# Moving the token shift of a windowed attention from TensorE to SP's transfers, with the mixture's fronts and the order of the stream set anew

## The chip, the cores and the metric

The kernel runs on one core of a Trainium2 chip. The core has five engines that run at the same time, each through its own instructions in a fixed order: PE (TensorE, matrix products and transposes), DVE (VectorE), ACT (ScalarE), POOL (GpSimd), and SP (SyncE), which here does nothing but issue transfers. An engine waits on semaphores where it needs what another produces. Transfers are carried out by 16 DMA engines beside them. The metric is the device time of one execution in microseconds (us).

## The reference, cut to what matters

The input `x` has 2 batch entries of 1024 tokens with 128 channels, float32. Six blocks follow each other, each added to `x`:

```python
x = x + 0.5 * L0_ffn(layernorm(x))    # mixture of 16 experts, two per token
x = x + L0_attn(layernorm(x))         # full attention, 16 heads of 64
x = x + 0.5 * L0_ffn(layernorm(x))    # the mixture again
x = x + 0.5 * L1_ffn(layernorm(x))    # two layers with windowed attention, below
x = x + L1_attn(layernorm(x))         # linear attention
x = x + 0.5 * L1_ffn(layernorm(x))    # the two layers again
```

The windowed block is what the change touches most. One of its layers reads

```python
def shift_token(t):
    t1, t2 = jnp.split(t, 2, axis=-1)
    t2 = jnp.pad(t2, ((0, 0), (1, 0), (0, 0)))[:, :-1]
    return jnp.concatenate([t1, t2], axis=-1)
...
h = shift_token(x)                    # q, k, v from h; rotary; windows of 64 tokens
x = x + local_attention(q, k, v) @ wo
h = shift_token(x)
h = (h - mean) / sqrt(var + 1e-5) * lg + lb
a, g = split(h @ w1 + b1)
x = x + (a * gelu(g)) @ w2 + b2
```

A token's shifted row has its own channels 0 to 63 and the channels 64 to 127 of the token before it (zeros for the first token of a batch entry). The shift of the second half of the layer is the one at issue.

## The kernel before, in words

**Layout.** `x` and `y` (the stream inside the windowed blocks) stay in SBUF as [128 tokens, 16 tiles, 128 channels], 8 tiles for each batch entry. A group is G = 4 tiles, so a batch entry has two groups (c = 0, 1). The windowed block runs twice, as `local("f0")` and `local("f1")`, with 2 layers x 4 groups each: 16 groups in all, so 16 shifts of the second kind.

**Stages.** First mixture and first attention take some 1000 us in an order that the change leaves alone. Beside the attention's steps POOL builds constants, one every few steps. Then comes the second mixture in 4 chunks of 512 tokens. A chunk has a front (`front_parts`: five pieces of the normalisation, `front_turned` L194, `front_kept` L199, `front_logits` L205, four pieces of `front_gates` from L210 on, `front_weights` L257 to L260) and nine pairs of experts (`entered` L284, `fetched` L292, `gated` L300, `multiplied` L304, `weighted` L308, `left` L268). The fronts of chunks 0 and 1 are done beside the end of the attention; those of chunks 2 and 3 lie in the stream described next.

**The stream.** From the second mixture on the order of all instructions comes from a list: `at(key, fn, ...)` (L950) enters a step with a number, the list is sorted by that number (L1619), and the steps are emitted in that order. Every engine takes its instructions in the order of emission; there is no scheduler behind it. So a table of numbers such as `per_group` is the order of each engine, and a step that is late holds back all that stands behind it on the same engine.

**A group in the windowed attention**, tile by tile: q and k are projected (`project`, L989), squared (L1002, ACT), multiplied by the rotary tables (`cosines` L1010 and `sines` L1021, DVE), summed and scaled (L1035, L1040, POOL), transposed (L1056), kept (L1062). `values` (L1067) and `valued` give v; `valued` stores the windows with two transfers on SP's queue (L1084, L1087: tile `vb` from `vo`). Scores (`attend`, L1100), mask, maximum, exponential, sums and weights (L1112 to L1139) follow, then the upright transposes (`upright`, L1147), the product with v (`weigh`, L1161), the projection (L1177) and the sum into `y` (`added`, L1183, DVE).

Four tiles done, the second half of the layer follows for the group. `lower_half` (L1191) copies channels 0 to 63 of `y` into a new tile `h` on POOL, and for c = 0 saves the last tile's upper channels as `late` for the next group. `shifted` (L1202 to L1205) does the shift on PE, by two or three products with matrices of ones and zeros, into a PSUM bank:

```python
nc.tensor.matmul(sp[:, 0:G, :], lhsT=down_one, rhs=ys[:, :, 64:C], ...)
if c > 0:
    nc.tensor.matmul(sp[:, 0, :], lhsT=last_first, rhs=late[l, b], ...)
nc.tensor.matmul(sp[:, 1:G, :], lhsT=last_first, rhs=ys[:, 0 : G - 1, 64:C], ...)
```

`upper_half` (L1209) copies the bank into `h` on ACT. Then h is normalised in five pieces (`norm_h`): moments on DVE (`bn_stats` L153, `bn_aggr` L155), the negative on POOL, the root on ACT, the offset on POOL, the application on ACT (L141). `inner_turned` (L1224) and what follows is the gated feed-forward, in whose end `outer_added` (L1288, DVE) adds its product `po` to `y`. Groups overlap: while group g is in its second half, the tiles of group g+1 are in their first.

Of the kernel before, what the change touches and what calls it, by code (L numbers as in the profile page):

```python
# [8 lines left out]
F32 = mybir.dt.float32  # L9
# [5 lines left out]
P = 128  # L15
B, S, C = 2, 1024, 128
# [4 lines left out]
NP = E // 2  # L21
# [10 lines left out]
def macaron_kernel(ctx: ExitStack, tc: tile.TileContext, a: dict, out: bass.AP):  # L32
# [835 lines left out]
    def first_weights():  # L868
# [6 lines left out]
        mask, mask0, causal, down_one, last_first = (  # L875
            w1a.tile([P, P], F32, name=nm) for nm in ("mask", "mask0", "causal", "down_one", "last_first")
# [20 lines left out]
                lambda: zero(down_one, 0.0),  # L897
                lambda: select(down_one, [[-1, P]], 1, 1, ne, 1.0),
                lambda: zero(last_first, 0.0),
                lambda: select(last_first[:, 0:1], [[0, 1]], -(P - 1), 1, ne, 1.0),  # L900

# [15 lines left out]
        shapes.extend([mask, mask0, causal, down_one, last_first, hblk, hgrp, hcol])  # L917

    attention0()
    mask, mask0, causal, down_one, last_first, hblk, hgrp, hcol = shapes  # L920
# [36 lines left out]
    def tiles_of(b, c):  # L957
        return b * TB + G * c
# [7 lines left out]
    def local(name, steps, normed, store):  # L966
# [221 lines left out]
        def lower_half(l, b, c):  # L1188
            ys = y[:, tiles_of(b, c) : tiles_of(b, c) + G, :]
            h = work.tile([P, G, C], F32, tag="h", name=f"h_{name}{l}{b}{c}")  # L1190
            nc.gpsimd.tensor_copy(h[:, :, 0:64], ys[:, :, 0:64])  # L1191
            if c == 0:
                late[l, b] = small.tile([P, 64], F32, tag=f"late{b}", name=f"late_{name}{l}{b}", bufs=1)
                nc.gpsimd.tensor_copy(late[l, b], ys[:, G - 1, 64:C])
            mids[l, b, c] = h

        def shifted(l, b, c):


            ys = y[:, tiles_of(b, c) : tiles_of(b, c) + G, :]  # L1200
            sp = ps_["h", l, b, c] = bankT(f"sh_{name}{l}{b}{c}").rearrange("p (k d) -> p k d", d=64)
            nc.tensor.matmul(sp[:, 0:G, :], lhsT=down_one, rhs=ys[:, :, 64:C], start=True, stop=False)  # L1202
            if c > 0:
                nc.tensor.matmul(sp[:, 0, :], lhsT=last_first, rhs=late[l, b], start=False, stop=False)
            nc.tensor.matmul(sp[:, 1:G, :], lhsT=last_first, rhs=ys[:, 0 : G - 1, 64:C], start=False, stop=True)  # L1205

        def upper_half(l, b, c):
            h = mids[l, b, c]
            nc.scalar.copy(h[:, :, 64:C], ps_.pop(("h", l, b, c))[:, 0:G, :])  # L1209
            mids[l, b, c] = h, norm_pieces(h, G, f"f{name}{l}{b}{c}", h)  # L1210
# [74 lines left out]
        def outer_added(l, b, c):  # L1285
# [5 lines left out]
            (-0.473, project), (-0.424, squares), (-0.249, cosines), (-0.183, sines), (0.096, least_norm),  # L1291
            (0.281, summed), (0.449, roots), (0.625, scaled), (0.834, turned), (0.880, kept),
            (1.214, attend), (1.218, masked), (1.742, lowered), (1.772, values), (1.865, valued),
            (2.038, raised), (2.216, totals), (2.464, weights), (2.737, upright), (2.777, stood),
            (3.084, weigh), (3.277, out_kept), (3.646, out_projected), (3.730, added),
        ]
        per_group = [
            (-0.203, lower_half), (0.205, shifted), (0.287, upper_half), (0.402, norm_h, 0),
            (0.701, norm_h, 2), (0.892, norm_h, 1), (1.199, norm_h, 3), (1.332, norm_h, 4),
            (1.625, inner_turned), (1.670, inner_kept), (2.276, second_bias), (2.397, gates),  # L1300
            (2.411, gelus), (2.511, third), (3.716, others), (3.934, first_two), (4.423, outer),
            (4.497, outer_added),
        ]
        for (l, b, c), n0 in steps.items():
            if l == 0:
                for part, d in enumerate(normed[b, c]):
                    at(d, norm, b, c, part)
            at(n0 - (0.786 if l == 0 else 2.722), channels, l, b, c)
            at(n0 + 0.749, keys_of_group, l, b, c)
            for k in range(G):  # L1310
                for d, fn in per_tile:
                    at(n0 + k + d, fn, l, b, G * c + k)
            for d, fn, *more in per_group:
                at(n0 + 7 + d, fn, l, b, c, *more)
            if l == 1:
                at(n0 + 11.568, onto_x, b, c, store)
# [16 lines left out]
    def linear_attention(starts):  # L1333
# [215 lines left out]
        def result(b, n):  # L1549
# [7 lines left out]
            (-0.327, norm, 0), (-0.133, norm, 1), (-0.117, norm, 2), (-0.075, norm, 3), (0.127, norm, 4),  # L1557
            (0.336, turned), (0.403, out_bias), (0.422, project, 2), (0.464, biased, 2),
            (0.504, project, 0), (0.568, biased, 0), (0.632, moments), (0.755, deviations),
            (0.874, inverted), (0.975, offsets),  # L1560
        ]
        per_tile = [
            (0.087, standard), (0.151, padded), (0.253, upright), (0.318, features), (0.374, spread),
            (0.592, keys_back), (0.620, scores, 1), (0.688, second_half), (0.890, cut), (1.118, scores, 0),
            (1.144, sums), (1.296, first_half), (1.303, summed), (1.407, numerators), (1.449, divided),
            (1.687, result), (2.068, moved),
# [13 lines left out]
    def mixture_at(chunks, fronts):  # L1580

        front_table = (
            -17.085, -13.072, -16.449, -1.888, 9.442, 10.794, 14.341, 21.404, 22.809, 28.561, 34.790,
            46.770, 47.680,
        )
        pair_table = [(1.440, fetched), (1.551, entered), (1.573, gated), (1.724, multiplied), (2.045, weighted), (2.197, left)]
        for c, m in chunks.items():
# [4 lines left out]
            at(m + 0.25 * NP + 2.388, finish, c)  # L1592
        for c, m in fronts.items():
            for d, (fn, *more) in zip(front_table, front_parts):
                at(m + d, fn, c, *more)
        return max(e[0] for e in plan)

    chunks = {0: -53.408, 1: -45.379, 2: 19.763, 3: 28.642}
    mixture_end = mixture_at(chunks, {2: -60.469, 3: -24.112})
    at(mixture_end + 0.001, moe_pool.close)  # L1600
    second = []
    at(-52.208, lambda: second.extend(later_weights()))
    at(-44.179, linear_weights)
    for k in range(4):
        at(20.581 + 0.3 * k, lambda k=k: table_scaled(*second, k))
    mixed = {g: [chunks[2 * g[0] + g[1]] + d for d in (4.394, 5.991, 11.199, 12.627, 13.589)] for g in groups}
    steps = {
        (0, 0, 0): 31.511, (0, 0, 1): 35.51, (0, 1, 0): 39.502, (0, 1, 1): 43.494,
        (1, 0, 0): 47.544, (1, 0, 1): 51.537, (1, 1, 0): 55.603, (1, 1, 1): 59.643,
    }  # L1610
    local("f0", steps, mixed, False)
    linear_attention({(0, 0): 59.504, (0, 1): 63.574, (1, 0): 67.587, (1, 1): 71.626})
    steps = {
        (0, 0, 0): 66.682, (0, 0, 1): 70.734, (0, 1, 0): 74.785, (0, 1, 1): 78.807,
        (1, 0, 0): 82.829, (1, 0, 1): 86.879, (1, 1, 0): 90.871, (1, 1, 1): 94.947,
    }
    mixed = {g: [steps[0, *g] + d for d in (-1.347, -1.236, -1.27, -1.04, -0.937)] for g in groups}
# [75 lines left out]
```

## Time and profile before

| what | value |
|---|---|
| median of 3 runs | 1915.93 us (1915.51 to 1917.19) |
| the profiled execution's own time | 1915.74 us |
| its span | 1913.7 us |
| PE, DVE, ACT, POOL busy | 96%, 73%, 59%, 59% of the span |
| mean granted clock of TensorE | 0.987 |

The span runs from the first to the last instruction of the profiled execution[...]. Times in a row of the profile are microseconds from the span's start unless marked ns. A row of the chain of waits has its start, how long it stood, the engine, the tile and the line of the source. A row of a timeline has start, duration, engine and line, and at its end in brackets how long the engine had idled and which instruction released it. A row of a table of stretches has the stretch, its length, the busy time of PE, weight loads, DVE, ACT and POOL (with the number of instructions), TensorE's granted clock as a share of full speed, the mean busy share of the 16 DMA engines (a sum over queues, so it can pass 1), and GB/s. A row of the transfers has the tiles, the queue, how often, the size of each and the median time from issue to landing; the rows for `vb` say 128.0 KB and about 2.2 us.

### The profile page before, as it was taken

The numbers are of one execution on the slowest core, as the hardware profiler recorded it, in microseconds if no ns is written. First come the engines' busy times: TensorE is split into PE (matmuls) and PEld (weight loads), VectorE is DVE, ScalarE is ACT, GpSimd is POOL, SyncE is SP. The second block draws the span as 40 slices with busy tenths as digits, with TensorE's granted clock in tenths as the row PEclk, the third lists the DMA queues.
The fourth block names the chain that finished last, engine by engine and source line by source line (L and its number), as shares of the span: only waits on it lengthen the run. The fifth ranks groups of instructions, "written<-read, shape, count | busy, mean of one in ns | idle before, by whom it ended". The sixth has DMA issues, their size and how long they took to land.

```text
span 1913.7 us, 37577 instructions
## 1 busy us (share of the span) xinstructions
PE 1837.6 (96%) x14482; PEld 1190.3 (62%) x14482; DVE 1401.8 (73%) x2450; ACT 1130.2 (59%) x2083; POOL 1135.1 (59%) x1036
## 2 busy tenths in 40 slices
PE   8999999999999999999999889999999899999997
PEld 5555666566665666656666556666756566666765
DVE  5748677776768677776763568888887788888884
ACT  4325555655566555655653356776767467677765
POOL 4544444343435444353344379888887689788883
PEclk8998999999999999999999899999999999999999
DMA  5330101010101001011023211111100000011110
GB/s 133 107 88 23 23 16 31 12 31 4 34 12 25 21 22 24 12 34 60 2 69 91 68 34 29 26 25 24 27 18 15 7 18 20 19 26 24 26 34 26
DMA packets 52413, 64.13 MB, mean 34 GB/s; under 512 B 17890, under 2 KB 26892, under 8 KB 51980
## 3 DMA queue, kind: packets, MB, share of 16 engines
q1 hardware_dynamic: 52236, 61.74, 12.6%
q8 instruction: 115, 1.88, 0.4%
q14 instruction: 62, 0.51, 0.1%
HBM read 27.89 MB, written 1.31 MB: 15 GB/s over the span
## 4 chain that ended last, share of the span: by engine, by line
PE 67%; DVE 12%; ACT 11%; POOL 4%; issue 4%; DMA 0%; SPq 0%; DVEq 0%; POOLq 0%; ACTq 0%
PE s L650 11%; PE tp L700 10%; PE av L717 9%; ACT p L679 3%; PE qk_f L989 3%; PE gu_m L284 2%; PE pq L598 2%; PE av_f L1161 2%; PE gu_m L285 2%; PE s_f L1100 2%; PE tp_f L1147 2%; PE tq_f L1056 2%; PE acc_m L268 2%; PE v_f L1067 2%; PE po_f L1277 2%
## 5 line engine op out<-in xcount | busy, mean ns | idle before, releaser
L686 POOL TENSOR_SCALAR p<-p,den 128x1024 f32<-128x1024 f32 x256 | 292.3, 1154 | 398.1 <-DVE den L684 316.5
L679 ACT ACTIVATE p<-p,nm 128x1024 f32<-128x1024 f32 x256 | 294.7, 1151 | 357.1 <-DVE nm L666 335.5
L666 DVE CUSTOM_DVE_ANT_0 p<-s,bias 128x1024 f32<-128x1024 f32 x256 | 302.8, 1220 | 103.7 <-PE s L650 102.3
L700 PEld LDWEIGHTS tp<-ident,p 128*128 128x128 f32 x2048 | 226.7, 141 | 99.3 <-issue 38.0
L700 PE MATMUL tp<-ident,p 128*128 128x128 f32 x2048 | 276.9, 278 | 11.7 <-ACT pt L704 10.3
L650 PE MATMUL s<-qk,qk 64*128 64x512 f32 x1024 | 258.3, 618 | 3.8 <-DVE nm L666 3.7
L717 PE MATMUL av<-pt,v 128*64 128x256 f32 x2048 | 249.0, 385 | 0.0
L706 DVE COPY pt<-tp 128x512 f32<-128x512 f32 x256 | 176.3, 689 | 92.6 <-PE tp L700 92.2
L717 PEld LDWEIGHTS av<-pt,v 128*64 128x64 f32 x2048 | 135.8, 136 | 150.1 <-issue 83.7
L1035 POOL TENSOR_TENSOR t_f<-t_f,t_f 128x1024 f32<-128x1024 f32 x64 | 151.0, 2360 | 15.3 <-DVE t_f L1021 12.5
L308 POOL TENSOR_TENSOR h_m<-h_m,cb_m 128x512 f32<-128x512 f32 x64 | 88.1, 1378 | 116.9 <-DVE h_m L304 88.1
L704 ACT COPY pt<-tp 128x512 f32<-128x512 f32 x256 | 147.4, 576 | 4.2 <-PE tp L700 3.9
L650 PEld LDWEIGHTS s<-qk,qk 64*128 64x128 f32 x1024 | 89.2, 186 | 88.3 <-issue 84.8
L1040 POOL TENSOR_TENSOR t_f<-t_f,rn_f 128x1024 f32<-128x1024 f32 x64 | 122.2, 1909 | 23.1 <-ACT rn_f L1031 19.6
L1139 POOL TENSOR_TENSOR s_f<-s_f,sm_f 128x1024 f32<-128x1024 f32 x64 | 121.4, 1898 | 15.9 <-DVE sm_f L1135 12.3
L989 PE MATMUL qk_f<-wqkv,hT 128*128 128x512 f32 x256 | 124.7, 610 | 2.5 <-DVE hh_f L1253 1.2
L1002 ACT ACTIVATE t_f<-qk_f 128x1024 f32<-128x1024 f32 x64 | 65.3, 1021 | 97.8 <-PE qk_f L989 90.4
L1125 POOL TENSOR_TENSOR s_f<-s_f,mx_f 128x1024 f32<-128x1024 f32 x64 | 121.9, 1905 | 0.4 <-DVE mx_f L1120 0.4
L300 ACT ACTIVATE h_m<-gu_m 128x512 f32<-128x512 f32 x72 | 43.0, 597 | 133.2 <-PE gu_m L285 126.5
L304 DVE TENSOR_TENSOR h_m<-h_m,gu_m 128x512 f32<-128x512 f32 x72 | 49.3, 685 | 83.9 <-ACT h_m L300 82.5
L1134 DVE TENSOR_REDUCE sm_f<-s_f 128x8 f32<-128x1024 f32 x64 | 77.9, 1217 | 26.7 <-ACT s_f L1130 26.6
L614 POOL TENSOR_TENSOR rot<-rot,rot 128x512 f32<-128x512 f32 x32 | 40.7, 1272 | 88.0 <-DVE rot L609 88.0
(376 smaller groups left out, 3762.6 us busy)
## 6 DMA issues: line engine op xcount, KB each, us to landing
cb_m<-cwd_m SPq DMA_DIRECT2D x128, 128.0 KB, 3.1
qk<-rot SPq DMA_DIRECT2D x256, 64.0 KB, 2.0
tab<-in_xpos_dram SPq DMA_DIRECT2D x2, 1024.0 KB, 6.7
wqkv<-in_L_ffn_wqkv_dram SPq DMA_DIRECT2D x2, 768.0 KB, 8.2
x<-in_L_attn_x_dram SPq DMA_DIRECT2D x4, 256.0 KB, 3.8
wraw<-in_qkv_wT_dram SPq DMA_DIRECT2D x2, 512.0 KB, 4.3
vb_f<-vo_f SPq DMA_DIRECT2D x8, 128.0 KB, 2.2
out_dram<-x SPq DMA_DIRECT2D x4, 256.0 KB, 2.3
```

Source lines behind the costliest of these rows:

```text
L650: nc.tensor.matmul(pss[r][:, c, :], lhsT=qT[rows[r], t * P : (t + 1) * P], rhs=kT[rows[r], c * 512 : (c + 1) * 512], start=True, stop=True,)
L666: nc.vector.tensor_tensor_reduce(out=s, in0=pss[r].rearrange("p a n -> p (a n)"), in1=bias[r][:, o : o + S], scale=-1.0, scalar=3.0e38, op ...
L679: nc.scalar.activation(s, s, AF.Exp, bias=nm[:, r : r + 1], scale=-1.0, accum_out=den[:, r : r + 1])
L686: nc.gpsimd.tensor_scalar(probs[i, r], probs[i, r], den[:, r : r + 1], 1.0, ALU.mult, ALU.mult)
L700: nc.tensor.transpose(tp[:, k * P : (k + 1) * P], s[:, kb * P : (kb + 1) * P], ident)
L704: nc.scalar.copy(dst, src)
L706: nc.vector.tensor_copy(dst, src)
L717: nc.tensor.matmul(po[r * 64 : r * 64 + 64, 0 : 2 * P], lhsT=v[:, kb, r * 64 : r * 64 + 64], rhs=pts[i // 2, r, g][:, kb - 4 * g, :], star ...
L989: nc.tensor.matmul(ps[:, s, :], lhsT=hTs[b][:, n * P : (n + 1) * P], rhs=lw[l][0][:, s * INNER : (s + 1) * INNER], start=True, stop=True,)
L1035: nc.gpsimd.tensor_tensor(t1, t1, t2, ALU.add)
L1040: nc.gpsimd.tensor_tensor(t3, t3, rn.unsqueeze(2).to_broadcast([P, 2 * HL, 64]), ALU.mult)
L1125: nc.gpsimd.tensor_tensor(s3, s3, mx.unsqueeze(2).to_broadcast([P, HL, P]), ALU.subtract)
```

## The change: what it does, and the diff

1. **The shift by transfers.** `shifted` has no matmuls any more. It issues transfers on SP's queue from `y` straight into `h`: one for rows 0 to 126 of all four tiles to rows 1 to 127 (127 rows, each 4 pieces of 64 floats), and three of a single row, each from the last row of a tile to the first row of the next. For c = 0 a fourth one-row transfer saves the last row of the group as `late`, now one row in place of 128. `lower_half` writes the first row's upper half on POOL: zeros for c = 0, a copy of `late` for c = 1. `upper_half` (the ACT copy) and the constants `down_one` and `last_first` are gone. The moments of h on DVE now read what the transfers write.

2. **The fronts of chunks 2 and 3** get a table of numbers each (`front_tables`) in place of one for both, and other starts. In the new order the transposes and logits of chunk 2 lie inside chunk 0 and its gates inside chunk 1. The four products that scale the second rotary table (`table_scaled`) move from the end of the mixture into chunk 0.

3. **The order of the stream**: the numbers of all tables and starts change: those of a tile and of a group in the windowed block, those of the pairs of experts, and those of the linear attention (where `project` 0 and 2 change places and `out_bias` moves behind the group).

```diff
-        mask, mask0, causal, down_one, last_first = (
-            w1a.tile([P, P], F32, name=nm) for nm in ("mask", "mask0", "causal", "down_one", "last_first")
+        mask, mask0, causal = (
+            w1a.tile([P, P], F32, name=nm) for nm in ("mask", "mask0", "causal")
...
-                lambda: zero(down_one, 0.0),
-                lambda: select(down_one, [[-1, P]], 1, 1, ne, 1.0),
-                lambda: zero(last_first, 0.0),
-                lambda: select(last_first[:, 0:1], [[0, 1]], -(P - 1), 1, ne, 1.0),
...
         def lower_half(l, b, c):
             ys = y[:, tiles_of(b, c) : tiles_of(b, c) + G, :]
             h = work.tile([P, G, C], F32, tag="h", name=f"h_{name}{l}{b}{c}")
             nc.gpsimd.tensor_copy(h[:, :, 0:64], ys[:, :, 0:64])
             if c == 0:
-                late[l, b] = small.tile([P, 64], F32, tag=f"late{b}", name=f"late_{name}{l}{b}", bufs=1)
-                nc.gpsimd.tensor_copy(late[l, b], ys[:, G - 1, 64:C])
+                nc.gpsimd.memset(h[0:1, 0, 64:C], 0.0)
+            else:
+                nc.gpsimd.tensor_copy(h[0:1, 0, 64:C], late.pop((l, b)))
             mids[l, b, c] = h
         def shifted(l, b, c):
             ys = y[:, tiles_of(b, c) : tiles_of(b, c) + G, :]
-            sp = ps_["h", l, b, c] = bankT(f"sh_{name}{l}{b}{c}").rearrange("p (k d) -> p k d", d=64)
-            nc.tensor.matmul(sp[:, 0:G, :], lhsT=down_one, rhs=ys[:, :, 64:C], start=True, stop=False)
-            if c > 0:
-                nc.tensor.matmul(sp[:, 0, :], lhsT=last_first, rhs=late[l, b], start=False, stop=False)
-            nc.tensor.matmul(sp[:, 1:G, :], lhsT=last_first, rhs=ys[:, 0 : G - 1, 64:C], start=False, stop=True)
-        def upper_half(l, b, c):
             h = mids[l, b, c]
-            nc.scalar.copy(h[:, :, 64:C], ps_.pop(("h", l, b, c))[:, 0:G, :])
+            nc.sync.dma_start(h[1:P, :, 64:C], ys[0 : P - 1, :, 64:C])
+            for k in range(1, G):
+                nc.sync.dma_start(h[0:1, k, 64:C], ys[P - 1 : P, k - 1, 64:C])
+            if c == 0:
+                late[l, b] = small.tile([1, 64], F32, tag=f"late{b}", name=f"late_{name}{l}{b}", bufs=1)
+                nc.sync.dma_start(late[l, b], ys[P - 1 : P, G - 1, 64:C])
             mids[l, b, c] = h, norm_pieces(h, G, f"f{name}{l}{b}{c}", h)
...
         per_tile = [
-            (-0.473, project), (-0.424, squares), (-0.249, cosines), (-0.183, sines), (0.096, least_norm),
-            (0.281, summed), (0.449, roots), (0.625, scaled), (0.834, turned), (0.880, kept),
-            (1.214, attend), (1.218, masked), (1.742, lowered), (1.772, values), (1.865, valued),
-            (2.038, raised), (2.216, totals), (2.464, weights), (2.737, upright), (2.777, stood),
-            (3.084, weigh), (3.277, out_kept), (3.646, out_projected), (3.730, added),
+            (-0.333, project), (-0.233, squares), (-0.062, cosines), (0.033, sines), (0.351, least_norm),
+            (0.495, summed), (0.600, roots), (0.610, scaled), (1.112, turned), (1.207, kept),
+            (1.382, attend), (1.387, masked), (1.866, lowered), (1.990, values), (2.070, valued),
+            (2.296, raised), (2.369, totals), (2.557, weights), (2.914, upright), (2.962, stood),
+            (3.272, weigh), (3.374, out_kept), (3.752, out_projected), (3.833, added),
         ]
         per_group = [
-            (-0.203, lower_half), (0.205, shifted), (0.287, upper_half), (0.402, norm_h, 0),
-            (0.701, norm_h, 2), (0.892, norm_h, 1), (1.199, norm_h, 3), (1.332, norm_h, 4),
-            (1.625, inner_turned), (1.670, inner_kept), (2.276, second_bias), (2.397, gates),
-            (2.411, gelus), (2.511, third), (3.716, others), (3.934, first_two), (4.423, outer),
-            (4.497, outer_added),
+            (-0.042, lower_half), (0.390, shifted), (0.555, norm_h, 0), (0.841, norm_h, 1),
+            (0.934, norm_h, 2), (1.040, norm_h, 3), (1.485, norm_h, 4), (1.705, inner_turned),
+            (1.778, inner_kept), (2.319, second_bias), (2.465, gates), (2.470, gelus), (2.636, third),
+            (3.811, others), (4.190, first_two), (4.443, outer), (4.514, outer_added),
         ]
...
-            at(n0 - (0.786 if l == 0 else 2.722), channels, l, b, c)
-            at(n0 + 0.749, keys_of_group, l, b, c)
+            at(n0 - (0.603 if l == 0 else 2.533), channels, l, b, c)
+            at(n0 + 0.476, keys_of_group, l, b, c)
...
-            (-0.327, norm, 0), (-0.133, norm, 1), (-0.117, norm, 2), (-0.075, norm, 3), (0.127, norm, 4),
-            (0.336, turned), (0.403, out_bias), (0.422, project, 2), (0.464, biased, 2),
-            (0.504, project, 0), (0.568, biased, 0), (0.632, moments), (0.755, deviations),
-            (0.874, inverted), (0.975, offsets),
+            (-0.593, norm, 0), (-0.389, norm, 1), (-0.305, norm, 2), (-0.300, norm, 3), (0.049, norm, 4),
+            (0.131, turned), (0.306, project, 0), (0.323, biased, 0), (0.326, project, 2),
+            (0.381, biased, 2), (0.402, moments), (0.704, deviations), (0.765, inverted), (0.852, offsets),
+            (4.923, out_bias),
         ]
...
-            (0.087, standard), (0.151, padded), (0.253, upright), (0.318, features), (0.374, spread),
-            (0.592, keys_back), (0.620, scores, 1), (0.688, second_half), (0.890, cut), (1.118, scores, 0),
-            (1.144, sums), (1.296, first_half), (1.303, summed), (1.407, numerators), (1.449, divided),
-            (1.687, result), (2.068, moved),
+            (0.005, standard), (0.025, padded), (0.100, upright), (0.106, features), (0.188, spread),
+            (0.339, keys_back), (0.358, scores, 1), (0.494, second_half), (0.831, cut), (0.913, scores, 0),
+            (0.986, sums), (1.067, first_half), (1.072, summed), (1.177, numerators), (1.262, divided),
+            (1.414, result), (1.662, moved),
...
-        front_table = (
-            -17.085, -13.072, -16.449, -1.888, 9.442, 10.794, 14.341, 21.404, 22.809, 28.561, 34.790,
-            46.770, 47.680,
-        )
-        pair_table = [(1.440, fetched), (1.551, entered), (1.573, gated), (1.724, multiplied), (2.045, weighted), (2.197, left)]
+        front_tables = {
+            2: (
+                -62.017, -18.403, -20.191, -0.510, 7.500, 7.530, 8.372, 8.638, 12.129, 16.836, 18.467,
+                19.130, 34.877,
+            ),
+            3: (
+                -35.776, -25.985, -21.812, -19.613, -19.522, -18.022, -16.920, -1.444, 1.143, 24.112,
+                35.239, 47.802, 49.373,
+            ),
+        }
+        pair_table = [(1.279, fetched), (1.757, entered), (1.809, gated), (1.974, multiplied), (2.189, weighted), (2.434, left)]
...
-            at(m + 0.25 * NP + 2.388, finish, c)
+            at(m + 0.25 * NP + 2.451, finish, c)
         for c, m in fronts.items():
-            for d, (fn, *more) in zip(front_table, front_parts):
+            for d, (fn, *more) in zip(front_tables[c], front_parts):
                 at(m + d, fn, c, *more)
...
-    chunks = {0: -53.408, 1: -45.379, 2: 19.763, 3: 28.642}
-    mixture_end = mixture_at(chunks, {2: -60.469, 3: -24.112})
+    chunks = {0: -78.234, 1: -67.717, 2: 6.506, 3: 16.874}
+    mixture_end = mixture_at(chunks, {2: -82.492, 3: -38.772})
...
-    at(-52.208, lambda: second.extend(later_weights()))
-    at(-44.179, linear_weights)
+    at(-77.034, lambda: second.extend(later_weights()))
+    at(-66.517, linear_weights)
     for k in range(4):
-        at(20.581 + 0.3 * k, lambda k=k: table_scaled(*second, k))
-    mixed = {g: [chunks[2 * g[0] + g[1]] + d for d in (4.394, 5.991, 11.199, 12.627, 13.589)] for g in groups}
+        at(-74.413 + 0.3 * k, lambda k=k: table_scaled(*second, k))
+    mixed = {g: [chunks[2 * g[0] + g[1]] + d for d in (10.407, 10.831, 13.054, 13.238, 13.609)] for g in groups}
     steps = {
-        (0, 0, 0): 31.511, (0, 0, 1): 35.51, (0, 1, 0): 39.502, (0, 1, 1): 43.494,
-        (1, 0, 0): 47.544, (1, 0, 1): 51.537, (1, 1, 0): 55.603, (1, 1, 1): 59.643,
+        (0, 0, 0): 20.06, (0, 0, 1): 24.042, (0, 1, 0): 28.015, (0, 1, 1): 31.989,
+        (1, 0, 0): 35.968, (1, 0, 1): 39.946, (1, 1, 0): 43.923, (1, 1, 1): 47.927,
...
-    linear_attention({(0, 0): 59.504, (0, 1): 63.574, (1, 0): 67.587, (1, 1): 71.626})
+    linear_attention({(0, 0): 48.19, (0, 1): 52.208, (1, 0): 56.18, (1, 1): 60.178})
...
-        (0, 0, 0): 66.682, (0, 0, 1): 70.734, (0, 1, 0): 74.785, (0, 1, 1): 78.807,
-        (1, 0, 0): 82.829, (1, 0, 1): 86.879, (1, 1, 0): 90.871, (1, 1, 1): 94.947,
+        (0, 0, 0): 54.923, (0, 0, 1): 58.922, (0, 1, 0): 62.917, (0, 1, 1): 66.916,
+        (1, 0, 0): 70.895, (1, 0, 1): 74.91, (1, 1, 0): 78.88, (1, 1, 1): 82.827,
...
-    mixed = {g: [steps[0, *g] + d for d in (-1.347, -1.236, -1.27, -1.04, -0.937)] for g in groups}
+    mixed = {g: [steps[0, *g] + d for d in (-1.236, -1.205, -1.002, -0.937, -0.686)] for g in groups}
```

## The prediction

> **What bounds the kernel.** I read the share of each engine first, then the span in stretches of 50 us, then the chain of work that ended last, and last the rows of the tiles that the change touches.
>
> ```profile
> PE 1837.6 (96%) x14482; PEld 1190.3 (62%) x14482; DVE 1401.8 (73%) x2450; ACT 1130.2 (59%) x2083; POOL 1135.1 (59%) x1036
> ...
> 1050.00:1100.00 50.00, 41.02 (x177) 25.87 (x178) 26.18 (x77) 17.15 (x35) 19.11 (x21) 0.86 0.21 65
> 1250.00:1300.00 50.00, 49.07 (x510) 34.25 (x504) 42.06 (x55) 34.61 (x64) 43.90 (x32) 1.00 0.09 22
> ```
>
> TensorE bounds nearly everything: 49 of 50 us in the windowed attention (1250 to 1300). The second mixture (1050 to 1100) is the exception: 41 of 50, at a granted clock of 0.86. In the windowed attention four token tiles (a group) take 41.2 us. The chain through one group:
>
> ```profile
> 1257.97 1.08 PE av_f L1161 x32
> 1259.06 0.63 PE sh_f L1202 x2
> 1259.69 0.33 PE sh_f L1205 x2
> 1260.01 1.03 PE s_f L1100 x32
> ```
>
> The shift matmuls are on it: 0.95 us here, and 1.18 us (1300.52 to 1301.70) in the second group of a batch entry, which has a third matmul. Were all sixteen on the path, their removal would give 8 x 0.95 + 8 x 1.18 = 17.0 us.
>
> **Part 1, the shift by transfers.** Per group: minus those matmuls, minus one ACT copy (0.37 us, off the chain), minus a 0.24 us POOL copy in half the groups, plus four transfers on SP's queue, plus one more for `late` in half of them: 72 issues. The first moves 127 rows of 4 x 256 B, 130 KB; the others one row each. A vb issue takes 0.46 us; 72 x 0.46 = 33 us of a queue that mostly waits; behind them stands only the vb pair of the next tile, a step of 10 us later. What counts is when they land, since DVE's moments of h (L153) now wait for them, and DVE works in order.
>
> ```profile
> 1257.75 0.46 SPq L1084 DMA_DIRECT2D vb_f0014n<-vo_f  x1
> 1258.32 0.54 SPq L1087 DMA_DIRECT2D vb_f0015n<-vo_f  x1
> ...
> 1263.51 0.86 DVE L153 BATCH_NORM_STATS2 st_ff<-h_f 128x6 f32<-128x128 f32 x4
> 1264.29 0.36 DVE L155 BATCH_NORM_AGGREGATE mv_ff<-st_ff 128x2 f32<-128x6 f32 x4
> 1264.57 0.66 DVE L1288 TENSOR_TENSOR y<-po_f,y 128x512 f32<-128x512 f32 x1
> 1266.57 0.29 DVE L1183 TENSOR_TENSOR y<-pj_f,y 128x128 f32<-128x128 f32 x1 [1.34 <-PE pj_f L1177]
> ```
>
> SP is free after the vb pair at 1258.86, so the big transfer starts then. In the new order L1288 goes ahead of L153. Moments, L1288 and the 1.34 us of idleness fill 1263.51 to 1266.57 = 3.06 us, and the moments take 1.14. So nothing is late if the transfer lands by 1266.57 - 1.14 = 1265.43, **6.6 us** after its issue; each us beyond delays L1183, then the cosines and sines (3.9 us more), POOL's sum and weights, and the upright transposes, for which PE already waits 0.67 us. That delay starts at ACT's copy of the values, before the shift on PE, so where it decides, the removed matmuls give nothing back.
>
> How long does the transfer take? No row has 127 rows. Nearest by size and kind is the store of the output, 512 packets: 2.3 us from issue to landing, about 1.0 of it moving. By that row it is in time. **Against it** speaks the Trainium skill, DMA: Bandwidth & Descriptors, section "Why a DMA increments its semaphore by 16 and not by 1": a transfer uses the largest number of engines up to 16 that divides its slowest dimension, and 127 is prime: one engine. Does this trace bear that out? Three stretches, the last two columns being the busy share of 16 DMA engines and GB/s:
>
> ```profile
> out_dram<-x SPq DMA_DIRECT2D x4, 256.0 KB, 2.3
> ...
> 1832.50:1832.60 0.10, 0.10 (x3) 0.10 (x2) 0.10 (x1) 0.10 (x2) 0.00 (x0) 1.00 0.94 297
> ...
> 999.65:999.75 0.10, 0.10 (x3) 0.10 (x2) 0.00 (x0) 0.10 (x1) 0.00 (x0) 1.00 0.37 113
> ...
> 9.50:10.00 0.50, 0.33 (x3) 0.22 (x2) 0.43 (x6) 0.17 (x1) 0.12 (x1) 0.61 1.35 217
> ```
>
> At 1832 the store of 128 rows keeps all engines busy. At 999.65 the 85 rows of w2 move alone: 0.37 of 16, and the packet records are five streams 23.5 ns apart. 5 is the largest divisor of 85 up to 16. I follow the rule, then. One engine's pace: 113 / 5 = 22.6 GB/s with 512 B packets, so 130 KB in 5.8 us; with the 256 B packets of Wg and Wu (9.5 us) 217 / 16 = 13.6 GB/s, so 9.6 us. I take 8.2, nearer the second for its packet size. With the store's 1.3 us that isn't moving: lands after **9.5 us** (7.1 to 10.9). The one-row transfers would queue on the same engine behind it.
>
> Late by 9.5 - 6.6 = 2.9 us in the plainest group. The same subtraction elsewhere, from the end of the values' copy and the vb issues before each L153: groups measured at 1223, 1263, 1305, 1346, 1387: 2.2, 2.9, 2.7, 3.7, 3.9; at 1662 to 1869 (six): 2.1, 2.9, 2.7, 3.7, 2.7, 2.8. Sum 32.3. At 1183, 1445, 1496 and 1607 SP is free 7 to 10 us ahead: some us of lateness against some us of PE, 0. The last group has no cover: before, L1183 to L153 took 1.81 us; now 9.5 plus about 0.1: +7.8. Together **+40** (11 at 7.1 us, 59 at 10.9). If the transfer were spread, the group sum would be -14.9 (17.0 less 0.95 and 1.18, the first group and the last), and the tail +2: three more issues and a landing in place of a matmul and a copy.
>
> The longer waits may cost clock as well. Rows of 3 us show 0.50 from 1059 to 1071, after PE had idled through most of 1053 to 1063, and 0.50 again at 1136, after 5.15 busy us of 9. The skill's TensorE: Matmul & The Clock Gate, Part 1, says one idle window of about 3.4 us halves the clock. By that rule waits of 1 to 2 us with work between cost nothing; by the row at 1136 they can cost 1.7 us a group, 24 in all. I take +4.
>
> **Part 2, the mixture's fronts.** Before, PE stands here:
>
> ```profile
> 1058.02 1.63 PE L194 MATMUL tp_m<-ident,xn_m 128*128 128x128 f32 x4 [4.15 <-ACT xn_m L141]
> ...
> 1063.14 1.02 PE L257 MATMUL cw_m<-ident,pr_m 128*16 128x128 f32 x4 [3.49 <-DVE pr_m L247]
> ```
>
> Chunk 2's gates run after chunk 1 (DVE 1054.9 to 1063.1), and chunk 3's normalisation stands on ACT behind two of y's. Then the slow clock: the third pair of chunk 2 starts at 1071.99. In the new order chunk 2's transposes and logits lie in chunk 0 and its gates in chunk 1. Chunk 1 gets two excursions to the log table in place of one; an excursion is two loads of 1.28 us and cost PE 0.8 us there. By ACT's order chunk 1's last gate ends near 1050.9; load 1.28 and roots 0.5; POOL's offset follows the last weighting (1053.3); apply 1.65, copy 0.58, chunk 3's logits 0.9: chunk 2 starts near 1056.9 instead of 1065.5. Its first gate waits for y's second normalisation, exp and a load, to 1060.2; its third pair starts near 1061.5 instead of 1072: -10.5. Part of the slow clock may stay: **-9.5** (-11 to -6). The four table products (1.27 us each on POOL) go between chunk 0's weightings, where POOL idles 1.35 of each 2.6 us: 0, and 5 without that cover.
>
> **Part 3, the order.** Sorted by key, the instructions of each engine in the steady groups follow each other as before, but for L1288 ahead of L153, POOL's small h steps a place earlier, and attend ahead of where the shift was. At the start of the windowed attention the moments of a later group (1.23 us of DVE at 1126.9) and a normalisation (1.64 us of ACT at 1127.8, behind which stands the key copy that PE waits 1.61 us for) move away: **-2** (-4 to 0). Around the linear attention projections are swapped and the output bias (1.27 us of POOL, four times) moves later; PE's waits from 1385 to 1550 are some 15 us, which can go either way: 0 (-5 to +5). The removed POOL constants ran beside the first attention under idle POOL: 0.
>
> **Sum** against the profiled execution (1915.74 us, span 1913.7; the median is 1915.93, the same): +40 + 4 - 9.5 - 2 = +32.5: **1948 us**.
>
> **Rivals.** (a) The transfer is **spread over many engines**, because the chip sees its dimensions otherwise than the rule has them: -15 + 2 - 9.5 - 2 = -24.5: **1891**, faster. For it: the store's row. Against it: the five streams. It decides as soon as the landing is under about 7 us, where lateness no longer outweighs parts 2 and 3. (b) One engine, but at the pace of the 512 B packets (7.1 us): +11 - 11.5 and a little clock: **1916**, about no change. (c) One engine slower than Wg's pace, or each group also loses clock: 59 + 24 - 11.5: **1987**. (d) The removed work wasn't on the path at all: refuted by the chain for most groups.
>
> **Numbers.** One engine and clearly late 0.72 (its own range 1920 to 1985); (a) 0.18; one engine and fast enough to be a gain 0.07, no change 0.03. A difference under 0.2% (4 us) cannot be told from none here. The range takes in (a)'s middle and leaves out its better half and what lies beyond (c): 1890 to 1987. Faster 0.25, same 0.03, slower 0.72.
>
> **What would show it.** The landing of h<-y (near 9.5 us or near 2.3); DVE waiting before L153 for that transfer, some 3 us in most groups; PE's wait before the upright transposes grown from 0.67 to above 3 us; a group of 44 us instead of 41; chunk 2 of the mixture starting 8 us earlier relative to chunk 0; a last group some 8 us longer. A landing below 7 us makes the forecast wrong in sign.

## The result, and the profile after

The changed kernel takes **1965.3 us** (median of 4 runs, 1964.1 to 1966.8) against 1916.6 us before (1915.5 to 1918.9): a ratio of 1.0258, 95% interval 1.0245 to 1.0270. It is 48.8 us slower; the forecast was 32.5 us slower (1948 us), with a range of 1890 to 1987. The profiled execution has a span of 1963.2 us, and the rest of this section compares it with the one before (1913.7).

The page of the changed kernel: the busy times, and the shares of the chain that ended last.

```profile
PE 1840.5 (94%) x14402; PEld 1193.4 (61%) x14402; DVE 1397.6 (71%) x2450; ACT 1129.7 (58%) x2069; POOL 1136.0 (58%) x1040
...
PE 59%; DVE 12%; ACT 10%; DMA 7%; POOL 7%; issue 5%; SPq 1%; DVEq 0%; ACTq 0%; POOLq 0%
```

The same shares of the kernel before:

```profile
PE 67%; DVE 12%; ACT 11%; POOL 4%; issue 4%; DMA 0%; SPq 0%; DVEq 0%; POOLq 0%; ACTq 0%
```

PE's busy time has grown by 2.9 us, though 80 matmul instructions are gone (14402 in place of 14482): the rest runs slower. Transfers stand in the chain with 7% of the span, some 140 us; before it was 0%. Two stretches of the span, the same two that the forecast shows of the kernel before, with the same columns (PE, weight loads, DVE, ACT, POOL, granted clock, DMA share, GB/s):

```profile
1050.00:1100.00 50.00, 47.00 (x217) 29.11 (x216) 25.34 (x69) 21.30 (x38) 18.44 (x19) 1.00 0.25 79
...
1250.00:1300.00 50.00, 44.98 (x436) 31.49 (x437) 38.38 (x51) 31.25 (x57) 39.73 (x30) 0.97 0.10 23
```

The mixture (1050 to 1100) has gained: 47 us of work in 50 where it had 41, and the full clock. The windowed attention has lost: 45 where it had 49, and a clock of 0.97. The chain through one group of it, restricted to 1300 to 1320 us (start, how long, what; three dots stand for rows left out):

```profile
1304.12 9.77 DMA h_f<-y
1313.88 0.03 issue
1313.91 0.02 DVEq L153
1313.93 0.04 issue
1313.98 0.87 DVE st_ff L153 x4
1314.85 0.29 DVE mv_ff L155 x4
1315.13 0.02 issue
1315.16 0.30 ACT rs_ff L162
...
1315.60 0.57 ACT pt_f L1147
1316.17 0.14 issue
1316.31 1.94 PE tq_f L1051 x8
```

The transfer holds up the moments of h on DVE; ACT's root (L162) waits for the moments; behind the root, in ACT's order, stand the copies of the transposed weights (L1147); and PE cannot write its next transposes (L1051) before those copies have emptied the bank. By the profile PE stands in this wait, for ACT's copies, behind shifts 0 to 4 and 9 to 12 (counted from 0 to 15 through both windowed blocks). Four engines' timelines at this place, SP, DVE, ACT and PE in turn:

```profile
1303.53 0.48 SPq L1082 DMA_DIRECT2D vb_f0101n<-vo_f  x1
1304.12 0.73 SPq L1199 DMA_DIRECT2D h_f<-y  x1
1304.90 8.35 SPq L1201 DMA_DIRECT2D h_f<-y  x3
...
1299.43 0.28 DVE L1178 TENSOR_TENSOR y<-pj_f,y 128x128 f32<-128x128 f32 x1
...
1308.56 0.68 DVE L1283 TENSOR_TENSOR y<-po_f,y 128x512 f32<-128x512 f32 x1
1313.98 0.87 DVE L153 BATCH_NORM_STATS2 st_ff<-h_f 128x6 f32<-128x128 f32 x4 [4.74 <-DMA h_f<-y]
...
1315.16 0.30 ACT L162 ACTIVATE rs_ff<-mv_ff,eps 128x4 f32<-128x4 f32 x1 [4.20 <-DVE mv_ff L155]
...
1302.09 1.04 PE L1051 MATMUL tq_f<-ident,t_f 128*128 128x128 f32 x8
...
1316.31 1.94 PE L1051 MATMUL tq_f<-ident,t_f 128*128 128x128 f32 x8 [3.85 <-ACT pt_f L1147]
```

The sum into y that the transfer needs (L1178) ended at 1299.71, 4.4 us before the issue at 1304.12: SP came to it only behind the `vb` pair. DVE then waits 4.74 us for the landing; over all sixteen shifts its waits for `h_f<-y` sum to 63.0 us, and in twelve of them it is 3.8 to 6.0 us. PE's wait is 3.85 us, and the transposes behind it take 1.94 us where the same eight took 1.04 us one tile earlier (1302.09). Stretches of 2 us say why:

```profile
1312.00:1314.00 2.00, 0.46 (x2) 0.00 (x0) 0.02 (x1) 0.00 (x0) 0.00 (x0) 1.00 0.08 14
1314.00:1316.00 2.00, 0.00 (x0) 0.00 (x0) 2.00 (x10) 0.81 (x3) 0.79 (x2) 0.87 0.00 0
1316.00:1318.00 2.00, 1.69 (x8) 1.57 (x8) 1.90 (x3) 1.70 (x4) 1.69 (x3) 0.50 0.02 4
1318.00:1320.00 2.00, 2.00 (x34) 1.79 (x32) 1.03 (x2) 1.56 (x3) 1.06 (x2) 0.50 0.56 131
1320.00:1322.00 2.00, 2.00 (x36) 1.59 (x32) 1.28 (x2) 1.79 (x5) 2.00 (x2) 0.50 0.00 0
1322.00:1324.00 2.00, 2.00 (x9) 0.99 (x6) 1.82 (x2) 0.66 (x3) 2.00 (x2) 0.93 0.00 0
```

After the pause the clock is 0.50 for 6.8 us (1315.5 to 1322.3 in the trace's record of the clock). Behind the six waits of shifts 0 to 5 (4.3, 3.2, 4.8, 3.9, 3.7 and 5.5 us) it is 0.50 for 3.4, 6.8, 3.4, 6.8, 3.4 and 6.8 us: the longer wait does not have the longer slow stretch. The transfer's packets (508 of 256 B) follow each other one at a time, some 15.7 ns apart, from about 1.4 to 9.4 us after the issue, in all sixteen groups.

In the mixture, PE's timeline at the place where it had waited 4.15 and 3.49 us:

```profile
1056.13 1.18 PE L194 MATMUL tp_m<-ident,xn_m 128*128 128x128 f32 x4
1057.15 0.60 PE L257 MATMUL cw_m<-ident,pr_m 128*16 128x128 f32 x4
1057.98 1.07 PE L205 MATMUL lg_m<-wr,xnT_m 128*128 128x16 f32 x8 [0.24 <-ACT xnT_m L199]
...
1063.74 1.12 PE L284 MATMUL gu_m<-xnT_m,wg 128*128 128x512 f32 x2 [1.16 <-DVE h_m L304]
```

Both waits are gone; the third pair of chunk 2 starts at 1063.74 in place of 1071.99.

### The profile page after: what moved, and what is told of

The parts are those of the page before. It is cut to its first block, busy times and chain, and to the rows that moved or that the text cites. A ratio compares the mean times of both kernels' runs of the same rounds, so it can differ in the third digit from the quotient of the medians.

```text
span 1963.2 us, 37628 instructions
## 1 busy us (share of the span) xinstructions
PE 1840.5 (94%) x14402; PEld 1193.4 (61%) x14402; DVE 1397.6 (71%) x2450; ACT 1129.7 (58%) x2069; POOL 1136.0 (58%) x1040
## 4 chain that ended last, share of the span: by engine, by line
PE 59%; DVE 12%; ACT 10%; DMA 7%; POOL 7%; issue 5%; SPq 1%; DVEq 0%; ACTq 0%; POOLq 0%
PE s L650 10%; PE tp L700 10%; PE av L717 9%; DMA h_f<-y 7%; ACT p L679 3%; PE gu_m L284 2%; PE gu_m L285 2%; PE pq L598 2%; PE qk_f L984 2%; PE av_f L1156 2%; PE acc_m L268 2%; POOL s_f L1120 2%; PE s_f L1095 2%; PE tq_f L1051 2%; PE ag_f L1234 1%
## 5 line engine op out<-in xcount | busy, mean ns | idle before, releaser
L1035 POOL TENSOR_TENSOR t_f<-t_f,rn_f 128x1024 f32<-128x1024 f32 x64 | 122.1, 1908 | 15.7 <-ACT rn_f L1026 14.7
L1051 PE MATMUL tq_f<-ident,t_f 128*128 128x128 f32 x512 | 74.9, 293 | 44.3 <-ACT pt_f L1147 34.7
L1051 PEld LDWEIGHTS tq_f<-ident,t_f 128*128 128x128 f32 x512 | 63.1, 151 | 84.8 <-POOL nb_ff L158 32.3
```

Source lines behind the costliest of these rows:

```text
L1051: nc.tensor.transpose(tp[:, j * P : (j + 1) * P], t1[:, o : o + P], ident)
```

## The experiments

**What is disputed.** Theory A, the forecast's: one DMA engine carries the 127 rows, and what waits for them costs the time. Theory B: the new order of the stream costs it. The first four kernels take the two apart.

**e1: the same transfer, cut so that more engines carry it.**

```diff
-            nc.sync.dma_start(h[1:P, :, 64:C], ys[0 : P - 1, :, 64:C])
+            nc.sync.dma_start(h[1:113, :, 64:C], ys[0:112, :, 64:C])
+            nc.sync.dma_start(h[113:P, :, 64:C], ys[112 : P - 1, :, 64:C])
```

> The changed kernel, but its 127-row transfer is cut into two, of 112 rows and of 15 rows (112 = 16 x 7, 15 = 15 x 1), everything else as it is. Theory A (the transfer runs on one DMA engine, lands some 9.4 us after its issue, and DVE, ACT and PE stand behind it): both parts land within 2.5 us, the moments of h no longer wait, TensorE keeps its full clock in the windowed attention, and the time is that of before, less 10.5 us from the mixture, less 14.9 us of shift matmuls, plus 2 us in the tail: 1893 us (1885 to 1902). Theory B (the new order of the stream is what costs, the transfers hardly matter): within 10 us of the changed kernel, 1955 to 1970 us.

Measured: 1895.0 us (1892.2 to 1898.5) against 1914.0 before, ratio 0.990 (0.9883 to 0.9917). Of e1, DVE at the same group and a stretch of the windowed attention:

```profile
1290.88 0.68 DVE L1284 TENSOR_TENSOR y<-po_f,y 128x512 f32<-128x512 f32 x1
1291.47 0.91 DVE L153 BATCH_NORM_STATS2 st_ff<-h_f 128x6 f32<-128x128 f32 x4
...
1250.00:1300.00 50.00, 49.43 (x527) 34.99 (x527) 43.45 (x63) 36.93 (x70) 44.18 (x36) 1.00 0.12 28
```

L153 follows L1284 with no wait, PE is full, and the clock is 1.00. A group takes 40.0 us (ends of L1284: 1251.56, 1291.56, 1331.55), where it took 41.2 before and some 46 in the changed kernel. One line of the kernel, cut in two, turns 49 us of loss into 19 us of gain: theory A, and B falls.

**e2: the shift on TensorE in the new order.** `lower_half`, `shifted`, `upper_half` and the two constants are as before; the rest is the changed kernel.

```diff
-            (-0.042, lower_half), (0.390, shifted), (0.555, norm_h, 0), (0.841, norm_h, 1),
+            (-0.042, lower_half), (0.280, shifted), (0.380, upper_half), (0.555, norm_h, 0), (0.841, norm_h, 1),
```

> The changed kernel with the shift put back on TensorE (matmuls, ACT copy, constants as before; shifted just ahead of attend, the copy just behind out_kept), in the new order and with the new fronts. Theory A: only the gain of the mixture is left, 1916.5 - 10.5 = 1906 us (1900 to 1912). Theory B: the loss stays, 1945 to 1970 us.

Measured: 1901.6 us (1901.4 to 1901.9), ratio 0.9933 (0.9917 to 0.995): 12.4 us faster than before. The new order is a gain, also without the transfers. Against e1 the removed matmuls are worth only 6.6 us, not the 13 of e1's expectation. By the ends of each group's last sum into y (of `po_f`), e1 gains about 1.1 us a group over e2, 5.3 us by the sixth group. By the eighth, the last of the first windowed block, it has given 4.9 of that back (2.2 in the trace of e9, which is the same kernel, so part of it belongs to the one execution); the second block gains again. Why the gain is given back there was not followed up.

**e3: the transfers in the old order.** The kernel before with the changed `lower_half` and `shifted`.

```diff
-            (-0.203, lower_half), (0.205, shifted), (0.287, upper_half), (0.402, norm_h, 0),
+            (-0.203, lower_half), (0.205, shifted), (0.402, norm_h, 0),
```

> The kernel before, with the shift by transfers as the changed kernel has it (127 rows in one), in the old order and with the old fronts. Theory A: the loss of the transfers without the mixture's gain, 1916.5 + 59 = 1975 us (1965 to 1990). Theory B: 1905 to 1930 us.

Measured: 1981.5 us (1976.2 to 1983.6), ratio 1.0347 (1.0328 to 1.0366): +67.5 us, 8 more than expected. Its DVE in a steady group:

```profile
1316.34 1.22 DVE L1116 TENSOR_REDUCE mx_f<-s_f 128x8 f32<-128x1024 f32 x1
1322.88 0.87 DVE L153 BATCH_NORM_STATS2 st_ff<-h_f 128x6 f32<-128x128 f32 x4 [5.31 <-DMA h_f<-y]
1323.67 0.36 DVE L155 BATCH_NORM_AGGREGATE mv_ff<-st_ff 128x2 f32<-128x6 f32 x4
1323.94 0.66 DVE L1284 TENSOR_TENSOR y<-po_f,y 128x512 f32<-128x512 f32 x1
```

In the old order the sum into y (here L1284, 0.66 us) stands behind L153 and waits too: 5.31 us of idleness in place of 4.74. By this one group the new order, which moves the sum ahead, helps by some 0.6 us; that step was not tried alone.

**e4: one engine, but issued ahead of the `vb` pair.**

```diff
-            (-0.042, lower_half), (0.390, shifted), (0.555, norm_h, 0), (0.841, norm_h, 1),
+            (-0.042, lower_half), (-0.030, shifted), (0.555, norm_h, 0), (0.841, norm_h, 1),
```

> The changed kernel; the only difference is the place of shifted in the order, 0.42 of a step earlier, ahead of the vb pair, so that the transfer can start when the last sum into y is there, some 4.4 us earlier. It still runs on one engine. Theory A, lateness alone: 4.4 of the 4.6 us for which DVE waits are covered, PE waits under 1 us and keeps its clock: 1903 us (1896 to 1920). Rival C (SP's queue: the next issue stands 7 us in the queue behind the 127-row transfer, and now the vb pair stands behind that): the vb pair comes some 8 us later and the product with v waits for it, 1935 to 1965 us.

Measured: 1904.1 us (1901.9 to 1904.5), ratio 0.9944 (0.993 to 0.9959). SP and DVE in the group of e1's lines, and DVE in the last group:

```profile
1282.01 0.73 SPq L1199 DMA_DIRECT2D h_f<-y  x1
1282.79 8.14 SPq L1201 DMA_DIRECT2D h_f<-y  x3
1291.04 0.53 SPq L1079 DMA_DIRECT2D vb_f0100n<-vo_f  x1
...
1291.62 0.88 DVE L153 BATCH_NORM_STATS2 st_ff<-h_f 128x6 f32<-128x128 f32 x4
...
1877.03 0.87 DVE L153 BATCH_NORM_STATS2 st_ff<-h_f 128x6 f32<-128x128 f32 x4 [7.02 <-DMA h_f<-y]
```

The transfer still takes 9.4 us, and L153 starts at 1291.62 against 1291.47 in e1: a slow transfer costs next to nothing in these groups if it is issued when its data is there. DVE's waits for `h_f<-y` sum to 10.0 us in place of 63.0, and 7.0 of them are the last group's. Rival C falls: the `vb` pair is issued at 1291.04, against 1285.22 in e1, and by the trace no product with v waits for it. What is left of the loss is the last group, where nothing covers the transfer: from the end of the 14th group's sum into y to that of the last, 49.5 us here, 42.6 in e1, 38.7 before.

**e5: what the slow clock costs.** In nine of the tiles in which PE waits, the product of v is done five times.

```diff
             pv = ps_["v", l, b, n] = bankO(f"v_{name}{l}{b}{n}", 0)
+            group = 4 * l + 2 * b + n // G
+            waits = n % G == 2 and group in ((3, 4, 5) if store else (1, 2, 3, 4, 5, 6))
-            nc.tensor.matmul(
+            for _ in range(5 if waits else 1):
+                nc.tensor.matmul(
```

> The changed kernel; in nine of the tiles in which TensorE waits for ACT behind the transfer (shifts 0 to 5 of the first windowed block and 2 to 4 of the second), the product of v ahead of the wait is done five times instead of once, into the same bank, so TensorE works through 3.5 us of a wait of 3.4 to 5.6 us. The four added products are wasted work. Theory A1 (the pause itself halves the clock for some 6 us behind it, which costs 2.6 us a group): the clock stays at 1.00 behind these nine waits and the time falls by 9 x 2.4 = 22 us, to 1943 us (1938 to 1950). Rival A2 (what follows the wait is slow because its operands come late, not because of the clock): no gain, 1963 to 1972 us. Rival A3 (the wait is not idle time that work can fill): 9 x 3.5 us longer, 1997 us.

Measured: 1952.8 us (1949.1 to 1957.4) against 1916.3 before, ratio 1.0201 (1.0183 to 1.0218). That is 36.5 us slower than before where the changed kernel was 48.8 slower: wasted work has made it some 12 us faster (the intervals of the two ratios leave 7 to 15). PE behind a filled wait, and the stretches there:

```profile
1260.90 4.46 PE L1065 MATMUL v_f<-wqkv,hT 128*128 128x512 f32 x10
1265.77 1.06 PE L1051 MATMUL tq_f<-ident,t_f 128*128 128x128 f32 x8 [0.41 <-ACT pt_f L1150]
...
1264.00:1266.00 2.00, 1.59 (x6) 0.55 (x5) 2.00 (x9) 1.35 (x5) 0.40 (x2) 1.00 0.01 0
1266.00:1268.00 2.00, 2.00 (x44) 1.76 (x46) 1.90 (x2) 2.00 (x5) 0.59 (x2) 1.00 0.12 31
```

The clock stays at 1.00 and the transposes take 1.06 us again. So A1's mechanism holds against A2 and A3. Its size was off, and the time lies above A1's range: 12.3 / 9 = 1.4 us a wait, not 2.4. At full clock PE soon waits for POOL's weights instead (0.58 us at 1272.77), so part of what the slow clock took was slack. The added products may have cost something themselves, so 1.4 us is what filling a wait gained, and the clock alone may cost a little more.

**e6: how the number of rows sets the pace.** Each group cuts the 127 rows in another way.

```diff
-            nc.sync.dma_start(h[1:P, :, 64:C], ys[0 : P - 1, :, 64:C])
+            for m in parts:
+                nc.sync.dma_start(h[1 + at_row : 1 + at_row + m, :, 64:C], ys[at_row : at_row + m, :, 64:C])
+                at_row += m
```

> The changed kernel with the 127 rows cut otherwise in each group, in turn: 127; 122 and 5; 124 and 3; 125 and 2; 119 and 8; 120 and 7; 121 and 6; 126 and 1; 64 and 63; 112 and 15; 96 and 31. Theory A (the number of engines is the largest divisor of the rows up to 16, and each engine takes 15.7 ns for a packet of 256 B): engines 1, 2, 4, 5, 7, 15, 11, 14, 16, 16, 16 for the first part, so 508, 244, 124, 100, 68, 32, 44, 36, 16, 28, 24 packets on the busiest of them, and 8.0, 3.8, 1.9, 1.6, 1.1, 0.5, 0.7, 0.6, 0.3, 0.4, 0.4 us from the first packet to the last. Rival D (the number of rows does not set the engines; it is the cut itself that helps): all the cut ones alike, 1 to 2 us. Time 1905 to 1925 us.

Measured in one execution (1906.2 us), from the trace's packet records, in us; expected is for the first part:

| rows | largest divisor up to 16 | expected | first to last packet |
|---|---|---|---|
| 127 | 1 | 8.0 | 8.0 |
| 122 + 5 | 2 | 3.8 | 3.8 |
| 124 + 3 | 4 | 1.9 | 1.9 |
| 125 + 2 | 5 | 1.6 | 1.5 |
| 119 + 8 | 7 | 1.1 | 1.2 |
| 121 + 6 | 11 | 0.7 | 1.0 |
| 126 + 1 | 14 | 0.6 | 0.8 |
| 120 + 7 | 15 | 0.5 | 1.1 |
| 64 + 63 | 16, then 9 | 0.3 | 2.3 |
| 112 + 15 | 16, then 15 | 0.4 | 1.9 |
| 96 + 31 | 16, then 1 | 0.4 | 2.6 |

The groups that repeat the first five cuts give 7.9, 3.8, 2.0, 1.5 and 1.2. Up to 14 engines the divisor sets the pace, and rival D falls: 122 rows and 124 rows differ by a factor of two. With 15 or 16 engines in the first part the whole takes longer again. The second part is issued 0.7 to 1.0 us later, and by the rule 31 rows run on one engine once more (124 packets, an estimate of 1.9 us). The place in the queue matters too: in e1 and in e9, both behind the `vb` pair, 112 + 15 takes 1.2 us in the same nine of sixteen groups and up to 2.5 in the other seven; in e8 and e10, which issue it ahead of that pair, it takes 1.2 us in all sixteen. Whether the pair holds up the engines or the queue these runs do not tell apart. SP's queue, for 127 rows, 122 + 5 and 124 + 3 (the parts, then the three single rows):

```profile
1166.95 0.81 SPq L1206 DMA_DIRECT2D h_f<-y  x1
1167.81 8.26 SPq L1209 DMA_DIRECT2D h_f<-y  x3
1212.88 3.58 SPq L1206 DMA_DIRECT2D h_f<-y  x2
1216.51 1.84 SPq L1209 DMA_DIRECT2D h_f<-y  x3
1253.45 1.81 SPq L1206 DMA_DIRECT2D h_f<-y  x2
```

The issue behind the large part stands 7.0 us in the queue after 127 rows, 2.8 after 122, 1.0 after 124: the fewer engines carry a transfer, the longer the next issue stands.

**e7: the mixture's fronts alone**, with the keys shifted by a constant to fit the old order (an extract).

```diff
-    chunks = {0: -53.408, 1: -45.379, 2: 19.763, 3: 28.642}
-    mixture_end = mixture_at(chunks, {2: -60.469, 3: -24.112})
+    chunks = {0: -66.783, 1: -56.266, 2: 17.957, 3: 28.325}
+    mixture_end = mixture_at(chunks, {2: -71.041, 3: -27.321})
...
-    mixed = {g: [chunks[2 * g[0] + g[1]] + d for d in (4.394, 5.991, 11.199, 12.627, 13.589)] for g in groups}
+    mixed = {g: [chunks[2 * g[0] + g[1]] + d for d in (10.407, 10.831, 13.054, 13.238, 13.609)] for g in groups}
```

> The kernel before with the mixture's new numbers alone (chunks, fronts, pairs, the second table's products), shifted by a constant so that the mixture ends where it did in the order; the windowed attention, the linear attention and the shift on TensorE as before. Theory A: the mixture's gain of 10.7 us alone, 1903 us (1900 to 1907), with the third chunk's end 10 to 11 us earlier. Rival E (part of the gain needs the new order behind it): 1907 to 1914 us.

Measured: 1906.4 us (1905.8 to 1908.0) against 1916.3, ratio 0.9952 (0.9937 to 0.9967): 9.9 us, and each group's last sum into y in its trace is 9.3 to 9.7 us earlier than before. The rest of the order, e2 less this, comes to some 2.5 us by the medians, but the two intervals overlap, so it is not clear of noise.

**e8, e9, e10: both cures.** e8 is e4 with e1's two transfers; e9 and e10 are e1 and e8 once more, side by side.

> The changed kernel with both: shifted ahead of the vb pair, and the 127 rows cut into 112 and 15. Theory A: the gain of the early issue through the linear attention (some 4 us more than the spread alone) with the short tail of the spread (7 us less than the early one alone): 1892 us (1887 to 1897). Rival: the two overlap in what they save, 1895 to 1904 us.

> The kernel of e1 once more (112 and 15 rows, the changed kernel's order), beside the next on the same chip, to tell the two apart. Theory A: 2 to 4 us above the next one, 1893 to 1897 us. Rival: no difference.

> The kernel of e8 once more (112 and 15 rows, issued ahead of the vb pair). Theory A: 1890 to 1894 us, 2 to 4 us below e9. Rival: the same as e9, since either lands before the moments of h could start anyway.

Measured: e8 1895.3 us (1893.5 to 1897.2), ratio 0.9893 (0.9878 to 0.9907); e9 1895.8 (1893.6 to 1897.9), ratio 0.9891; e10 1894.7 (1894.2 to 1899.0), ratio 0.9892. The hoped-for 2 to 4 us of issuing early as well are not there: the medians of e9 and e10 are 1.1 us apart, and their runs overlap. Either cure alone covers the steady groups; spreading the rows also shortens the tail. e1 is the version to keep: 1.1% faster than the kernel before, 3.5% faster than the changed one (1895.8 against 1965.3).

## Why the prediction was right, and where it was short

The sign, the mechanism and the range were right; the size fell short by 16 us. To place the shortfall, take the end of the last sum into y of each group, after less before, from stretch to stretch, for the changed kernel and for e5, in which nine waits kept their clock (the profiled executions; a plus is slower):

| stretch | forecast | changed kernel | e5 |
|---|---|---|---|
| mixture (end of chunk 3) | -9.5 | -9.7 | -11.3 |
| start of the windowed attention, shift 0 (filled) | -2 | +2.4 | +1.7 |
| shifts 1 to 5 (filled) | +15.4 | +22.9 | +15.4 |
| shifts 6 to 8, linear attention | 0 | -0.3 | -1.6 |
| shifts 9 to 13 (10 to 12 filled) | +14.1 | +18.2 | +14.6 |
| shifts 14 and 15, tail | +10.6 | +16.0 | +14.8 |
| clock, everywhere | +4 | in the rows above | in the rows above |
| sum | +32.6 | +49.5 | +33.6 |

"Filled" marks the waits that e5 filled. The 1.6 us between the last two columns in the first row are there already at the mixture's first matmul, ahead of anything that e5 changes.

- **Part 1, the landing: right.** 9.5 us (7.1 to 10.9) was forecast from the divisor rule and the pace of 256 B packets; the last packet ended 9.2 to 9.5 us after the issue, and the row of the chain has the landing 9.77 us after it. The rule of the Trainium skill (DMA: Bandwidth & Descriptors, "Why a DMA increments its semaphore by 16 and not by 1") was a better guide than the row of the output's store (2.3 us), and the five streams of the 85-row transfer had shown which to believe; e6 bears it out closely from 1 to 7 engines, and within 0.3 us at 11 and 14.
- **Part 1, the lateness: right in size, not in its path.** Shifts 1 to 5 sum to 15.4 us in the forecast and to 15.4 us in e5; that they agree to the tenth is luck, since single groups differ by up to 0.9 us. The forecast looked for a wait of more than 3 us before the upright transposes, behind cosines and POOL. Those wait less than before: from 1100 to 1480 us 10.9 us for POOL's weights, against 19.4. The 3.85 us stand before the next transposes, of q and k, behind ACT's root and copies. DVE held back ACT as well as its own line of work.
- **Part 1, the clock: this step failed.** "I take +4" from a bound of 0 to 24. The forecast itself expected PE to wait above 3 us, but judged the clock by "waits of 1 to 2 us", and so read the Trainium skill's rule of one idle window of about 3.4 us (TensorE: Matmul & The Clock Gate, Part 1) as costing nothing. The measured waits are long enough by that rule, or nearly so, and the clock fell behind each. In the traces of all the kernels here, from 1000 us on, TensorE waits 2.7 us or more 32 times, and each time the clock is 0.50 by 1.1 us after the wait's end at the latest; of 17 waits of 2.0 to 2.4 us it fell behind five. Two of the 32 (2.69 us in e3, 3.23 us in the changed kernel) are shorter than the rule's window, so here less was enough. The price is 11.8 us in the three rows with filled waits and 12.3 us by the medians, 1.3 to 1.4 us a wait, near the 1.7 that the row at 1136 had given as the upper end. By this price the twelve groups with a slow stretch (shifts 0 to 5 and 10 to 15) come to about 16 us, an estimate, in place of 4: most of the shortfall.
- **Part 1, shift 0 and the tail: too small.** The forecast had SP free 7 to 10 us before L153 of the first group and took 0; in the changed kernel DVE comes to L153 5.8 us after the issue and waits 4.06 us. For the end +7.8 and, for shift 14, +2.8 were taken; both together cost 16.0, of which about 3 us are the clock again by the price above.
- **Part 2, the fronts: right.** -9.5 forecast, -9.7 in the trace, -9.9 in e7. The third pair of chunk 2 was to start at 1061.5 and starts at 1063.74. Chunk 2 itself starts at 1058.90 in place of 1056.9, since chunks 0 and 1 end 2.1 and 3.3 us later than before (1.7 of it at the mixture's first matmul already: 990.91 against 989.22).
- **Part 3, the order: not decided.** -2 forecast, about -2.5 by e2 less e7, which is not clear of noise. Around the linear attention 0 was taken, -0.3 found.
- **Rivals.** Rival (a), spread over many engines, was priced at 1891; e1, which makes it so, measures 1895.0. The landing bound of about 7 us from which it was to decide is met there (last packet after 2.5 to 3.9 us). Its sum counted -14.9 us for the matmuls, of which the difference of e1 and e2 has 6.6 us left at the end. Rival (b)'s pace was too fast: 15.7 ns for 256 B are 16 GB/s, not 22.6. Of rival (c), 1987, half came true: the groups lost clock, at a landing near the forecast's. Rival (d) falls with e1's shorter group (40.0 us, against 41.1 in e2, which has the matmuls).

## What to carry to other kernels

Before moving a copy from an engine to a transfer, factor its number of rows: here 127 rows went one packet at a time and took 8 us, 112 + 15 took 1.2 to 2.5. Then ask what stands in front of it in its queue: the same slow transfer, issued when its data was ready and not behind the next pair in the queue, cost nothing where other work covered it. And where a wait on a full TensorE comes to 3 us or more, count the half clock behind it as well as the wait: some 1.4 us each in this kernel.

## What was not expected of the hardware

An issue on SP's queue stood 7.0 us behind the 127-row transfer, though it was for a single row: a transfer on few engines holds up the queue, and not only its readers. And work without use made the kernel faster: 36 repeated products, filling nine waits of 3.2 to 5.5 us, saved some 12 us.
